# Layer 0 of a four-layer network: VectorE's second operands in PSUM, and the side work of the loop cut into other steps

## The chip, the cores and the metric

The kernel runs on one core of one Trainium2 chip. The metric is the device time of one execution in microseconds (us), lower is better. A core has TensorE (PE, matmuls), VectorE (DVE), ScalarE (ACT), GpSimd (POOL) and queues that start transfers. [...]SBUF is the main on-chip memory[...].

## The reference

The input x has the shape (2, 512, 32, 32). Four layers follow each other. Layer 0 is deformable attention with a position bias, then an MLP; layer 1 is a linear attention, layers 2 and 3 are attention with a group norm. The change touches layer 0 alone. Cut to what matters of it:

```python
xn = bn(x)                                   # (b, 512, 32, 32)
q = gconv1x1(xn, qw)                         # 8 groups of 64 channels
off = depthwise_conv6x6(q, stride 4)         # (b*8, 64, 8, 8): 36 taps
off = tanh(einsum(gelu(off + b), pw)) * 4
vgrid = 2 * (grid + off) / 7 - 1             # 64 sampling points for each group
kv = grid_sample(xn, vgrid)                  # bilinear
k, v = gconv1x1(kv, kw), gconv1x1(kv, vw)
pos = grid_q[:, :, None] - vgrid[:, None]    # 1024 queries x 64 points x 2
bias = sign(pos) * log1p(abs(pos))
bias = relu(bias @ w1 + b1)                  # 2 -> 128
bias = relu(bias @ w2 + b2)                  # 128 -> 128
bias = bias @ w3 + b3                        # 128 -> 1
attn = softmax(q.T @ k * scale + bias)
x = x + out_w @ (attn @ v) + out_b
```

## The kernel before, in words

The heavy part of layer 0 is the bias MLP: 16 heads (2 images x 8) x 1024 queries x 64 points through a 128x128 layer. It runs in a loop over 256 rounds, `quads`: 16 heads `u`, 8 steps `o`, 2 halves `jj`. A round covers four points of a head with all 1024 queries. Below, a round with jj = 0 is called even, one with jj = 1 odd. A pair is two heads that share the 128 partitions; there are eight pairs, so 32 rounds each.

In every round, in this order of the program:

1. `first_hidden` for the *next* round: VectorE writes four tiles' halves `h` of 128 x 1024 (L455, a custom add with saturation, of a row term `x` in SBUF and a column term `y` in PSUM). Every second time, for an even round to come, `table` first writes new `y` (L443). `h` has four buffers of two such halves, so two rounds' worth.
2. `second_hidden` for this round: PE makes four products `hp` (L486), each 128 x 1024 in two PSUM banks of a pool `ps` with three slots. ScalarE takes each out with Relu (L491), ScalarE and GpSimd flip signs (L493, L495, L497, L502), and GpSimd adds them (L504) or starts adding transfers (L478).
3. In even rounds `last_product`: the third layer's product for a pair of rounds that lies back (`sim`, L518).
4. The two queues of side work each take one step, up to the next `yield` of a generator: `after` holds the attention of finished heads (`attend`: ss, then tp with maximum and subtraction, exp, sum with inverse and product, pp/pt, o) and the output projection; `front` holds the preparation of the next pair (`offsets`: xn, q, products with the taps, their reduction `conv`, gelu, tanh, positions, logarithms; `sampled`: transposes, the weights `w` of the sampling, kv, keys and values).

The order on PE, ScalarE, VectorE and GpSimd is that of the program (`manual_schedule`), so a step's instruction stands behind the h of its round, and before the h of the next one.

`bank` is a tile of one PSUM bank, 512 values for each partition. It holds `y` (0 to 256), and for moments the small products: `o` of the offsets (L309, read by tanh, L311), `kv_ps` (L376), `k_ps` and `v_ps` (L389, L391, read at L394 to L397). Lines that the prediction names besides: L263 xn, L281 the copies of q, L288 the products with the taps, L301 their reduction, L352 to L357 the step that makes the distances g, wx and w, L367 to L370 the step that makes the weights of w, L541 ss, L550 and L551 maximum and subtraction, L555 to L557 sum, inverse and product, L565 pt, L617 and L621 the projection.

Of the kernel before, what the change touches and what calls it, by code (L numbers as in the profile page):

```python
# [11 lines left out]
F32 = mybir.dt.float32  # L12
# [40 lines left out]
class Net:  # L53
# [43 lines left out]
    def layer0(self):  # L97
# [3 lines left out]
        with ExitStack() as ctx:  # L101
            keep = self.pool(ctx, "l0")
            self.l0qkv = keep.tile([P, 3, CT, P], F32, tag="qkv", name="qkv")
            nc.scalar.dma_start(self.l0qkv[:, 0], io["l0_qkv"][:, 0])
            nc.scalar.dma_start(self.grid, io["grid"])
            self.l0w2 = keep.tile([P, P], F32, tag="w2", name="w2")
            nc.scalar.dma_start(self.l0w2, io["cpb_w2"])
            self.s1 = self.bn(keep, "bn1")
            self.last_weights(keep)
            nc.scalar.dma_start(self.l0qkv[:, 1:3], io["l0_qkv"][:, 1:3])  # L110
            ow = keep.tile([P, CT, C], F32, tag="ow", name="ow")
            nc.scalar.dma_start(ow, io["out_w"])
# [12 lines left out]
            self.bank = self.pool(ctx, "c_ps_t", 1, psum=True).tile([P, HF], F32, tag="bank", name="bank")  # L125
            ps_s = self.pool(ctx, "c_ps_s", 1, psum=True)

            engines = {getattr(mybir.EngineType, e) for e in ("PE", "Activation", "DVE", "Pool")}
            with self.tc.manual_schedule(engines=engines):
                pairs = [{} for _ in range(BP)]  # L130
                for n, _ in enumerate(self.offsets(pairs[0], 0, ps)):
                    if n == 4:
                        self.fold_weights()
                front = [self.sampled(pairs[0], 0, ps)]
                after, sims, att = [], {}, None
                tables = {}
                quads = [(u, o, jj) for u in range(2 * BP) for o in range(8) for jj in range(2)]
                ready = self.first_hidden(*quads[0], pairs, tables)
                held, self.join = [], None
                for i, (u, o, jj) in enumerate(quads):  # L140
                    if o == 1 and jj == 1 and u % 2 == 0 and u // 2 + 1 < BP:
                        nxt = pairs[u // 2 + 1]
                        front += [self.offsets(nxt, u // 2 + 1, ps), self.sampled(nxt, u // 2 + 1, ps)]
                    h1 = ready
                    if i + 1 < len(quads):
                        if quads[i + 1][1:] == (7, 0) and u + 1 < 2 * BP:
                            self.advance(front, lambda: "logs" in pairs[(u + 1) // 2])
                        ready = self.first_hidden(*quads[i + 1], pairs, tables)
                    z = self.second_hidden(u, o, jj, h1, i + 1 == len(quads))
                    if jj == 1:  # L150
                        held.append((u, o, (first, z)))
                    else:
                        first = z
                        if len(held) == 2:
                            v, last, zs = held.pop(0)
                            self.last_product(v, last, zs, sims, ps_s)
                            if last == 7:
                                if v % 8 == 0:
                                    self.advance(after, lambda: False)
                                    att = [  # L160
                                        apool.tile([P, N], F32, tag=f"att{t}", name=f"att{v}_{t}") for t in range(CT)
                                    ]
                                self.advance(front, lambda: "v" in pairs[v // 2])
                                after.append(self.attend(v, pairs[v // 2], sims.pop(v), att, ps))
                                if v % 8 == 7:
                                    after.append(self.projection(ps, att, ow, v // 8))
                    self.step(after)
                    self.step(front)

                self.join(True)  # L170
                self.advance(after, lambda: False)
                self.last_product(*held[0], sims, ps_s)
                accs = [ps.tile([P, 2, HF], F32, tag="ps", name=f"ob{o}") for o in range(CT - 1)]
                share = self.share(accs, att, ow)
# [59 lines left out]
    def step(behind):  # L234

        while behind:
            for _ in behind[0]:
                return
            behind.pop(0)

    @staticmethod
    def advance(behind, enough):

        while behind and not enough():
            for _ in behind[0]:
                break
# [2 lines left out]

    def projection(self, ps, att, ow, b):  # L250
        for o in range(CT):
            for h in range(2):
                self.project_one(ps, att, ow, "out_b", b, o, h)
                yield

    def offsets(self, m, bt, ps):

# [29 lines left out]
        for ky in range(6):  # L287
# [7 lines left out]
                self.colr("dw_w", len(TAPS))[:, 6 * ky : 6 * ky + 6].unsqueeze(2).unsqueeze(3).to_broadcast([P, 6, 8, 8]),  # L295
                ALU.mult,
            )
            if ky % 3 == 2:
                yield
        conv = self.fpool.tile([P, NJ], F32, tag="conv", name=f"conv{b}{t}")  # L300
        nc.vector.tensor_reduce(conv, prod.rearrange("p a b j -> p j (a b)"), AX.X, ALU.add)  # L301
        yield
        ge = self.fpool.tile([P, NJ], F32, tag="ge", name=f"ge{b}{t}")
        nc.scalar.activation(ge, conv, AF.Gelu, bias=self.col("dw_b"))
        yield
        o = self.bank[:, 256:258]
        for par in range(2):
            rows = slice(par * DH, (par + 1) * DH)
# [27 lines left out]
    def sampled(self, m, bt, ps):  # L336
# [11 lines left out]
        for n in range(NB):  # L348
# [8 lines left out]
        nc.vector.tensor_tensor(  # L357
            w,
            g[:, 1, :].unsqueeze(1).to_broadcast([P, NB, 2 * NJ]),
            self.grid[:, G_Y : G_Y + NB].unsqueeze(2).to_broadcast([P, NB, 2 * NJ]),  # L360
            ALU.subtract,
        )
        yield
        nc.scalar.activation(wx, wx, AF.Abs)
        nc.scalar.activation(w, w, AF.Abs)
        yield
        nc.vector.tensor_scalar(wx, wx, -1.0, 1.0, ALU.mult, ALU.add)  # L367
        nc.vector.tensor_scalar(wx, wx, 0.0, None, ALU.max)
        nc.vector.tensor_scalar(w, w, -1.0, 1.0, ALU.mult, ALU.add)
        nc.vector.scalar_tensor_tensor(w, w, 0.0, wx.unsqueeze(1).to_broadcast([P, NB, 2 * NJ]), ALU.max, ALU.mult)  # L370
        yield
        kv_ps = self.bank[:, 384:448]
        for n in range(NB):
            for par in range(2):
# [13 lines left out]
        k_ps = self.bank[:, 448:512]  # L388
        nc.tensor.matmul(k_ps, lhsT=self.l0qkv[:, 1, t, :], rhs=kv, start=True, stop=True)  # L389
        v_ps = self.bank[0:NJ, 256:384]  # L390
# [135 lines left out]
    def attend(self, u, m, sim, att, ps):  # L526
# [22 lines left out]
        e = self.soft.tile([P, 8, NJ], F32, tag="e", name=f"e{u}")  # L549
        nc.vector.tensor_reduce(st[:, 0, :], tp, AX.X, ALU.max)  # L550
        nc.vector.tensor_tensor(e, tp, st[:, 0, :].unsqueeze(2).to_broadcast([P, 8, NJ]), ALU.subtract)  # L551
        yield
        nc.scalar.activation(e, e, AF.Exp)
        yield
        nc.vector.tensor_reduce(st[:, 1, :], e, AX.X, ALU.add)  # L555
        nc.vector.reciprocal(st[:, 2, :], st[:, 1, :])
        nc.vector.tensor_tensor(e, e, st[:, 2, :].unsqueeze(2).to_broadcast([P, 8, NJ]), ALU.mult)  # L557
        yield
        pp = ps.tile([P, HF], F32, tag="ps", name=f"pp{u}") if ps else self.bank
        for i in range(4):  # L560
            nc.tensor.transpose(
# [987 lines left out]
```

## Time and profile before

| | |
|---|---|
| median of 3 executions | 3453.95 us (3453.79 to 3456.14) |
| profiled execution, span | 3450.1 us |
| TensorE busy | 3394.9 us, 98% |
| VectorE busy | 2313.2 us, 67% |
| ScalarE busy | 2017.4 us, 58% |
| GpSimd busy | 2078.3 us, 60% |
| between 86 and 2066 us (most of layer 0): PE busy | 1975.24 of 1980 us |
| the same stretch: DVE, ACT, POOL busy | 1435.56, 1540.08, 1526.80 us |
| TensorE clock granted | 0.997 |

A line of the groups reads: line of the kernel, engine, operation, output<-input by the program's names, shape, number of records | busy us, mean ns of one | idle time just before them, and what ended most of it. A line of a timeline reads: start us, duration us, engine, line, operation, names, shapes, number of records merged, and in brackets idle time before it with its releaser. A matmul of fp32 leaves two records. The ends of matmuls are modelled: a PE that waits for an operand within a group is drawn as a longer group, which is why the starts are compared.

### The profile page before, as it was taken

What the parts mean: (1) busy time and instruction counts of PE and PEld (TensorE: products, weight loads), DVE (VectorE), ACT (ScalarE), POOL (GpSimd) and SP (SyncE); (2) the same over time, 40 slices, a digit from 0 to 9 for tenths busy, and PEclk for the clock granted to TensorE, in tenths of its full rate; (3) what the DMA queues carried; (4) which work ended last, traced back from release to release, by engine and by line L of the source; (5) the groups of instructions that cost most, each with busy time, mean ns of one, the idle gap of its engine ahead of it and who ended that gap; (6) DMA issues with size and microseconds to landing.
All of it is one profiled execution on the core that took longest, in us unless ns stands there. A gap on an engine that the chain in (4) does not pass through costs nothing.

```text
span 3450.1 us, 60119 instructions
## 1 busy us (share of the span) xinstructions
PE 3394.9 (98%) x25280; PEld 1260.6 (37%) x25280; DVE 2313.2 (67%) x2539; ACT 2017.4 (58%) x2100; POOL 2078.3 (60%) x1584
## 2 busy tenths in 40 slices
PE   7999999999999999999999999999999999999999
PEld 2333333333333333333333334444555433455333
DVE  6877777777767567777776764575556577555774
ACT  5877877887787577877887761111111466113661
POOL 4778777787787577787788874442323444234441
PEclk9999999999999999999999999999989999999999
DMA  6878777877887577887888872111000100000001
GB/s 154 156 144 159 149 155 146 156 158 141 157 161 141 108 156 149 155 157 144 167 168 158 159 152 76 49 37 37 1 1 0 50 1 2 1 0 13 2 1 50
DMA packets 103247, 342.64 MB, mean 99 GB/s; under 512 B 12720, under 2 KB 14384, under 8 KB 100144
## 3 DMA queue, kind: packets, MB, share of 16 engines
q0 software_dynamic: 73296, 266.90, 41.0%
q1 hardware_dynamic: 28656, 69.68, 6.8%
q8 instruction: 202, 3.31, 0.4%
q10 hardware_dynamic: 1008, 2.06, 0.2%
q14 instruction: 85, 0.70, 0.1%
HBM read 67.27 MB, written 4.46 MB: 21 GB/s over the span
## 4 chain that ended last, share of the span: by engine, by line
PE 80%; DVE 15%; ACT 2%; POOL 1%; issue 1%; DMA 0%; DVEq 0%; ACTq 0%; SPq 0%; POOLq 0%
PE hp L486 46%; DVE h L455 3%; PE pb L598 3%; DVE r L1298 3%; PE sim L518 3%; PE o L1275 2%; DVE sum L1262 2%; PE s L1246 2%; PE qk20P L1041 1%; PE qk30P L1041 1%; PE m_0P L649 1%; PE qk21P L1041 1%; PE m_5P L649 1%; PE m_4P L649 1%; PE m_2P L649 1%; PE qk31P L1041 1%
## 5 line engine op out<-in xcount | busy, mean ns | idle before, releaser
L486 PE MATMUL hp<-h,w 128*32 128x512 f32 x16384 | 1831.1, 593 | 5.5 <-DVE h L455 3.6
L455 DVE CUSTOM_DVE_ANT_1 h<-tx,bank 128x1024 f32<-128x1024 f32 x1024 | 1180.4, 1215 | 332.9 <-PE hp L486 310.6
L491 ACT ACTIVATE h<-hp,magb 128x1024 f32<-128x1024 f32 x1024 | 1122.0, 1111 | 416.7 <-PE hp L486 415.6
L486 PEld LDWEIGHTS hp<-h,w 128*32 128x32 f32 x16384 | 543.1, 110 | 1216.1 <-issue 1120.9
L478 POOL DMA_DIRECT2D h<-h x509 | 451.7, 1023 | 392.5 <-ACT h L497 334.0
L504 POOL TENSOR_TENSOR h<-h,h 128x1024 f32<-128x1024 f32 x255 | 613.5, 2406 | 21.3
L502 POOL TENSOR_SCALAR h<-h,flip 128x1024 f32<-128x1024 f32 x256 | 447.7, 1749 | 0.9 <-ACT h L491 0.9
L1250 ACT ACTIVATE e<-s 128x1024 f32<-128x1024 f32 x256 | 258.2, 1024 | 177.6 <-PE s L1246 164.1
L493 ACT ACTIVATE h<-h,flip 128x1024 f32<-128x1024 f32 x256 | 291.3, 1138 | 0.0
L1275 PE MATMUL o<-e,v 64*64 64x512 f32 x2048 | 261.0, 592 | 6.7 <-DVE q L1285 6.7
L1246 PE MATMUL s<-q,k 64*64 64x512 f32 x2048 | 259.8, 589 | 2.6 <-DVE v L1079 1.8
L1257 POOL TENSOR_TENSOR some<-some,e 128x1024 f32<-128x1024 f32 x64 | 151.5, 2367 | 75.7 <-ACT e L1250 73.3
L495 POOL TENSOR_SCALAR h<-h,flip 128x1024 f32<-128x1024 f32 x128 | 144.9, 1132 | 77.4 <-ACT h L491 76.0
L1255 POOL TENSOR_TENSOR some<-e,e 128x1024 f32<-128x1024 f32 x32 | 75.5, 2361 | 190.8 <-DVE sum L1264 155.6
L497 ACT ACTIVATE h<-h,flip 128x1024 f32<-128x1024 f32 x128 | 145.6, 1137 | 0.0
L518 PE MATMUL sim<-h,ends 128*32 128x512 f32 x1024 | 141.0, 592 | 0.0
L1260 DVE TENSOR_TENSOR sum<-e,e 128x1024 f32<-128x1024 f32 x32 | 46.4, 1451 | 136.1 <-ACT e L1250 136.1
L1275 PEld LDWEIGHTS o<-e,v 64*64 64x64 f32 x2048 | 75.8, 133 | 157.3 <-issue 123.7
L1246 PEld LDWEIGHTS s<-q,k 64*64 64x64 f32 x2048 | 78.7, 133 | 143.4 <-issue 117.9
L628 POOL TENSOR_TENSOR mlp_w<-mlp_w 128x512 f32<-128x512 f32 x16 | 22.4, 1401 | 161.0 <-DMA mlp_w<-in_mlp_w 136.7
L708 ACT ACTIVATE mh<-mh,cols 128x512 f32<-128x512 f32 x64 | 46.2, 722 | 124.2 <-DVE mh L726 65.5
L1029 POOL TENSOR_TENSOR sq<-q 128x512 f32<-128x512 f32 x32 | 33.3, 1039 | 139.7 <-DVE q L1048 95.6
(456 smaller groups left out, 3280.2 us busy)
## 6 DMA issues: line engine op xcount, KB each, us to landing
h<-h POOLq DMA_DIRECT2D x509, 512.0 KB, 6.5
lb<-logs SPq DMA_DIRECT2D x63, 512.0 KB, 5.2
mlp_w<-in_mlp_w SPq DMA_DIRECT2D x16, 1024.0 KB, 4.9
x<-in_x SPq DMA_DIRECT2D x8, 512.0 KB, 9.7
qkw<-in_l_qk SPq DMA_DIRECT2D x2, 2048.0 KB, 8.3
out<-x SPq DMA_DIRECT2D x16, 256.0 KB, 2.1
vw<-in_l_v SPq DMA_DIRECT2D x2, 1024.0 KB, 7.4
proj<-in_l_proj SPq DMA_DIRECT2D x8, 256.0 KB, 5.1
```

Source lines behind the costliest of these rows:

```text
L455: self.nc.vector._custom_dve(TENSOR_ADD_SAT, out=h[:, k, :, :], in0=x[:, jj, 2 * r + k, :].unsqueeze(1).to_broadcast([P, H, W]), in1=y[:, ...
L478: nc.gpsimd.dma_start(to, what, accum_op=ALU.add)
L486: nc.tensor.matmul(hp[rows, cut], lhsT=self.l0w2[:, 32 * q : 32 * q + 32], rhs=h1[k][:, cut], start=True, stop=True)
L491: nc.scalar.activation(y, hp, AF.Relu, bias=self.magb[:, q : q + 1])
L493: nc.scalar.activation(ys[0], ys[0], AF.Copy, scale=self.flip[:, 0:1])
L502: nc.gpsimd.tensor_scalar(y, y, self.flip[:, 2:3], 1.0, ALU.mult, ALU.mult)
L504: (nc.vector if final else nc.gpsimd).tensor_tensor(y, y, ys[2], ALU.add)
L518: nc.tensor.matmul(sims[u][at : at + 32, :], lhsT=self.ends[:, 28 - 4 * o : 60 - 4 * o], rhs=z[jj][:, h * HF : (h + 1) * HF], start=(o == ...
L1246: nc.tensor.matmul(s[halves[c], par, :], lhsT=ks[p][rows, at : at + DH], rhs=qs[p][rows, cut], start=True, stop=True)
L1250: nc.scalar.activation(e, s, AF.Exp, scale=DH**-0.5)
L1257: nc.gpsimd.tensor_tensor(state["some"], state["some"], e, ALU.add)
L1275: nc.tensor.matmul(o[halves[par], r, :], lhsT=v[n // 2][rows, n % 2, at : at + DH], rhs=e[rows, par, :], start=(n == 0), stop=(n == NB - 1),)
```

## The change

Five things are edited.

- Operands of VectorE that both lay in SBUF: one of each pair now lies in free columns of `bank`. The taps (36 columns) and the row numbers `ys` (8) are copied there once; `inv`, the inverse of the softmax's sum, and `wp`, the weights along x, are written there by the instruction that makes them. `k_ps` and `v_ps` move to other columns to make room.
- The convolution in parts: the products go two rows of taps to a step instead of three, and their reduction is cut into three instructions with a step each. The last step of the weights `w` is cut in two.
- Two of the attention's steps (those with the maximum and with the sum) give back True, and so does the projection; in such a round the front queue takes no step.
- `odd()`: three steps that use the bank from PE wait, by empty yields, for a round with jj = 1. `advance`, which runs steps in bulk, sets jj to 1 so that it doesn't spin.
- The projection takes both halves of a block in one step with one addition of 1024 columns.

The purpose is that VectorE doesn't wait for GpSimd[...], and that its long steps don't meet in one round. Cut to its core:

```diff
+            self.taps, self.ys = self.bank[:, 320 : 320 + len(TAPS)], self.bank[:, 356 : 356 + NB]
+            self.inv = self.bank[:, 364 : 364 + 8]
+            nc.vector.tensor_copy(self.taps, self.colr("dw_w", len(TAPS)))
+            self.jj = 1
...
-                    if n == 4:
+                    if n == 7:
+                        nc.vector.tensor_copy(self.ys, self.grid[:, G_Y : G_Y + NB])
                         self.fold_weights()
...
+                    self.jj = jj
...
-                    self.step(after)
-                    self.step(front)
+                    if not self.step(after):
+                        self.step(front)
...
-            for _ in behind[0]:
-                return
+            for much in behind[0]:
+                return much
...
+    def odd(self):
+        while self.jj == 0:
+            yield
...
     def projection(self, ps, att, ow, b):
         for o in range(CT):
+            acc = ps.tile([P, 2, HF], F32, tag="ps", name=f"out_b{b}{o}")
             for h in range(2):
-                self.project_one(ps, att, ow, "out_b", b, o, h)
-                yield
+                for t in range(CT):
+                    self.nc.tensor.matmul(acc[:, h, :], ...)
+            self.nc.vector.scalar_tensor_tensor(xt, acc, self.col("out_b", o), xt, ALU.add, ALU.add)
+            yield True
...
-                self.colr("dw_w", len(TAPS))[:, 6 * ky : 6 * ky + 6].unsqueeze(2)...
+                self.taps[:, 6 * ky : 6 * ky + 6].unsqueeze(2)...
-            if ky % 3 == 2:
+            if ky % 2:
                 yield
-        nc.vector.tensor_reduce(conv, prod.rearrange("p a b j -> p j (a b)"), AX.X, ALU.add)
-        yield
+        for third in (slice(0, 24), slice(24, 44), slice(44, NJ)):
+            nc.vector.tensor_reduce(conv[:, third], prod[:, :, :, third].rearrange("p a b j -> p j (a b)"), AX.X, ALU.add)
+            yield
...
+        yield from self.odd()
...
-            self.grid[:, G_Y : G_Y + NB].unsqueeze(2)...
+            self.ys.unsqueeze(2)...
...
+        nc.vector.tensor_scalar(w, w, -1.0, 1.0, ALU.mult, ALU.add)
+        yield
+        wp = self.bank[:, 384:512]
         nc.vector.tensor_scalar(wx, wx, -1.0, 1.0, ALU.mult, ALU.add)
-        nc.vector.tensor_scalar(wx, wx, 0.0, None, ALU.max)
-        nc.vector.tensor_scalar(w, w, -1.0, 1.0, ALU.mult, ALU.add)
-        nc.vector.scalar_tensor_tensor(w, w, 0.0, wx.unsqueeze(1)..., ALU.max, ALU.mult)
+        nc.vector.tensor_scalar(wp, wx, 0.0, None, ALU.max)
+        nc.vector.scalar_tensor_tensor(w, w, 0.0, wp.unsqueeze(1)..., ALU.max, ALU.mult)
...
         nc.vector.tensor_tensor(e, tp, st[:, 0, :]..., ALU.subtract)
-        yield
+        yield True
...
-        nc.vector.reciprocal(st[:, 2, :], st[:, 1, :])
-        nc.vector.tensor_tensor(e, e, st[:, 2, :]..., ALU.mult)
-        yield
+        inv = self.inv if ps else st[:, 2, :]
+        nc.vector.reciprocal(inv, st[:, 1, :])
+        nc.vector.tensor_tensor(e, e, inv..., ALU.mult)
+        yield True
```

More of the change, by code (lines that the diff above doesn't have):

```diff
@@ L236, in step, with advance @@
         while behind:
-            for _ in behind[0]:
-                return
+            for much in behind[0]:
+                return much
             behind.pop(0)
-    @staticmethod
-    def advance(behind, enough):
+    def odd(self):
+        while self.jj == 0:
+            yield
+    def advance(self, behind, enough):
+        self.jj = 1
         while behind and not enough():
@@ L251, in projection @@
         for o in range(CT):
+            acc = ps.tile([P, 2, HF], F32, tag="ps", name=f"out_b{b}{o}")
             for h in range(2):
-                self.project_one(ps, att, ow, "out_b", b, o, h)
-                yield
+                for t in range(CT):
+                    self.nc.tensor.matmul(
+                        acc[:, h, :],
+                        lhsT=ow[:, t, o * P : (o + 1) * P],
+                        rhs=att[t][:, h * HF : (h + 1) * HF],
+                        start=(t == 0),
+                        stop=(t == CT - 1),
+                    )
+            xt = self.xs[b][o].rearrange("p (h x) -> p h x", h=2)
+            self.nc.vector.scalar_tensor_tensor(xt, acc, self.col("out_b", o), xt, ALU.add, ALU.add)
+            yield True
     def offsets(self, m, bt, ps):
@@ L294, in offsets @@
                 ),
-                self.colr("dw_w", len(TAPS))[:, 6 * ky : 6 * ky + 6].unsqueeze(2).unsqueeze(3).to_broadcast([P, 6, 8, 8]),
+                self.taps[:, 6 * ky : 6 * ky + 6].unsqueeze(2).unsqueeze(3).to_broadcast([P, 6, 8, 8]),
                 ALU.mult,
             )
-            if ky % 3 == 2:
+            if ky % 2:
                 yield
         conv = self.fpool.tile([P, NJ], F32, tag="conv", name=f"conv{b}{t}")
-        nc.vector.tensor_reduce(conv, prod.rearrange("p a b j -> p j (a b)"), AX.X, ALU.add)
-        yield
+        for third in (slice(0, 24), slice(24, 44), slice(44, NJ)):
+            nc.vector.tensor_reduce(conv[:, third], prod[:, :, :, third].rearrange("p a b j -> p j (a b)"), AX.X, ALU.add)
+            yield
         ge = self.fpool.tile([P, NJ], F32, tag="ge", name=f"ge{b}{t}")
@@ L359, in sampled @@
             g[:, 1, :].unsqueeze(1).to_broadcast([P, NB, 2 * NJ]),
-            self.grid[:, G_Y : G_Y + NB].unsqueeze(2).to_broadcast([P, NB, 2 * NJ]),
+            self.ys.unsqueeze(2).to_broadcast([P, NB, 2 * NJ]),
             ALU.subtract,
@@ L366, in sampled @@
         yield
+        nc.vector.tensor_scalar(w, w, -1.0, 1.0, ALU.mult, ALU.add)
+        yield
+        wp = self.bank[:, 384:512]
         nc.vector.tensor_scalar(wx, wx, -1.0, 1.0, ALU.mult, ALU.add)
-        nc.vector.tensor_scalar(wx, wx, 0.0, None, ALU.max)
-        nc.vector.tensor_scalar(w, w, -1.0, 1.0, ALU.mult, ALU.add)
-        nc.vector.scalar_tensor_tensor(w, w, 0.0, wx.unsqueeze(1).to_broadcast([P, NB, 2 * NJ]), ALU.max, ALU.mult)
+        nc.vector.tensor_scalar(wp, wx, 0.0, None, ALU.max)
+        nc.vector.scalar_tensor_tensor(w, w, 0.0, wp.unsqueeze(1).to_broadcast([P, NB, 2 * NJ]), ALU.max, ALU.mult)
         yield
+        yield from self.odd()
         kv_ps = self.bank[:, 384:448]
@@ L387, in sampled @@
         yield
-        k_ps = self.bank[:, 448:512]
+        yield from self.odd()
+        k_ps = self.bank[:, 256:320]
         nc.tensor.matmul(k_ps, lhsT=self.l0qkv[:, 1, t, :], rhs=kv, start=True, stop=True)
-        v_ps = self.bank[0:NJ, 256:384]
+        v_ps = self.bank[0:NJ, 384:512]
         nc.tensor.matmul(v_ps, lhsT=kv, rhs=self.l0qkv[:, 2, t, :], start=True, stop=True)
@@ L555, in attend @@
         nc.vector.tensor_reduce(st[:, 1, :], e, AX.X, ALU.add)
-        nc.vector.reciprocal(st[:, 2, :], st[:, 1, :])
-        nc.vector.tensor_tensor(e, e, st[:, 2, :].unsqueeze(2).to_broadcast([P, 8, NJ]), ALU.mult)
-        yield
+        inv = self.inv if ps else st[:, 2, :]
+        nc.vector.reciprocal(inv, st[:, 1, :])
+        nc.vector.tensor_tensor(e, e, inv.unsqueeze(2).to_broadcast([P, 8, NJ]), ALU.mult)
+        yield True
         pp = ps.tile([P, HF], F32, tag="ps", name=f"pp{u}") if ps else self.bank
```

## The prediction

> **What bounds the kernel now.** I read the busy shares, then the chain that ended last, then the costliest groups, and last the timelines of single engines inside layer 0.
>
> ```profile
> PE 3394.9 (98%) x25280; PEld 1260.6 (37%) x25280; DVE 2313.2 (67%) x2539; ACT 2017.4 (58%) x2100; POOL 2078.3 (60%) x1584
> PE 80%; DVE 15%; ACT 2%; POOL 1%; issue 1%; DMA 0%; DVEq 0%; ACTq 0%; SPq 0%; POOLq 0%
> L486 PE MATMUL hp<-h,w 128*32 128x512 f32 x16384 | 1831.1, 593 | 5.5 <-DVE h L455 3.6
> L455 DVE CUSTOM_DVE_ANT_1 h<-tx,bank 128x1024 f32<-128x1024 f32 x1024 | 1180.4, 1215 | 332.9 <-PE hp L486 310.6
> ```
>
> TensorE holds the whole kernel, and layer 0 above all. VectorE's time counts only where TensorE waits for it. The busy share hides that: a matmul that waits for its operand is drawn as a long one. In the chain's own order an undisturbed pair of rounds of the 256-round loop takes 14.59 us (128 hp records 13.73, 8 sim records 0.86), one round's 64 hp records 6.87 to 7.07. The excess over that is the stall. The timelines of PE, then VectorE (DVE), then GpSimd (POOL), at a pair's second collision:
>
> ```profile
> 340.99 0.66 PE L561 MATMUL pp<-ident,e 128*128 128x128 f32 x4
> 341.71 10.36 PE L486 MATMUL hp<-h,w 128*32 128x512 f32 x64
> 351.99 0.66 PE L576 MATMUL o<-pt,v 64*64 64x256 f32 x8
> 360.76 8.24 PE L486 MATMUL hp<-h,w 128*32 128x512 f32 x62
> ```
> ```profile
> 333.96 1.92 DVE L557 TENSOR_TENSOR e<-e,st 128x512 f32<-128x512 f32 x1
> 335.81 4.63 DVE L288 TENSOR_TENSOR prod<-qpad,cols 128x384 f32<-128x384 f32 x3
> 340.35 4.61 DVE L455 CUSTOM_DVE_ANT_1 h<-tx,bank 128x1024 f32<-128x1024 f32 x4
> ...
> 352.97 4.40 DVE L301 TENSOR_REDUCE conv<-prod 128x64 f32<-128x2304 f32 x1
> ```
> ```profile
> 333.57 1.76 POOL L502 TENSOR_SCALAR h<-h,flip 128x1024 f32<-128x1024 f32 x1
> 335.42 2.71 POOL L504 TENSOR_TENSOR h<-h,h 128x1024 f32<-128x1024 f32 x1
> ```
>
> 64 hp records take 10.36 instead of 7.0: 3.4 us lost. VectorE was late with h: e x st (L557, shortest 0.69) took 1.92 beside L502, and three products (L288, shortest 0.82) took 4.63 beside L504. At 360.76 the 4.40 us convolution costs another 1.5, and 0.64 went ahead of the 3.4, where the q copies waited behind ACT's exp. I added such excesses from 90 to 2089 us: 4.8 in pair 0 and 1 (0.94 + 0.84 + 2.98), then 5.6, 5.5, 5.6, 4.6, 5.6, 5.6 for the six later pairs: **37.1 us**. That is all that the change can win inside the loop.
>
> The 2.98 is the case that I use most below. Round 19 has the attention's tp step and the corner weights' step together; hp began at S = 192.0:
>
> ```profile
> 192.84 0.69 DVE L551 TENSOR_TENSOR e<-tp,st 128x512 f32<-128x512 f32 x1
> 193.45 0.39 DVE L367 TENSOR_SCALAR wx<-wx 128x128 f32<-128x128 f32 x1
> 193.88 2.42 DVE L368 TENSOR_SCALAR wx<-wx 128x128 f32<-128x128 f32 x1
> 196.22 0.68 DVE L369 TENSOR_SCALAR w<-w 128x1024 f32<-128x1024 f32 x1
> 196.94 1.23 DVE L370 SCALAR_TENSOR_TENSOR w<-w,wx 128x1024 f32<-128x1024 f32 x1
> 198.08 4.61 DVE L455 CUSTOM_DVE_ANT_1 h<-tx,bank 128x1024 f32<-128x1024 f32 x4
> ```
> ```profile
> 192.00 1.76 POOL L502 TENSOR_SCALAR h<-h,flip 128x1024 f32<-128x1024 f32 x1
> 193.84 2.38 POOL L504 TENSOR_TENSOR h<-h,h 128x1024 f32<-128x1024 f32 x1
> ```
>
> L367 slips in when L502 ends; L368 (0.23 when free) then sits out all of L504. It isn't a pair of tensors: it has one SBUF tensor.
>
> [...]3.02 for a product's longest, 2.42 for L368, while L551, with an operand in PSUM, is 690 to 692 ns in all its 15 runs. [...]So tensor_scalar from SBUF stays exposed, and the change doesn't touch that. [...]L357 shows 1225 to 1226. With PSUM in it L455 takes 1214, so moving an operand has no price of its own.
>
> **The budget of a round.** h for round i+2 can be written only when hp of round i is done, and must be there when hp of i+1 is. Work that waits for PE's last matmul of round i (pt, ss, tp, q) starts at S, the start of the next hp. Until the next hp PE has 7.0 us plus its own step work (0.6 for tp or o) plus 0.86 for sim, if the coming round is even. VectorE needs 4.65 for four h, and 0.45 for L443 if the coming round is odd. That leaves about 2.5 us after an even round and 3.1 or more after an odd one. Work that doesn't wait for S starts some 2.4 earlier.
>
> **The change part by part.** I walked both queues (attention, front) through the 256 rounds by the order of their yields.
> - Operands in PSUM: 48 products, 8 w subtractions, 8 w products, 16 e x inv lose the lock wait. Their floors stay (0.82, 1.23, 1.23, 0.69). The products read every fourth element, which the operand's move leaves as it is. VectorE saves 48 x (1.19 - 0.82) = 18 us, all of it only of use where PE waits.
> - Products two at a time, the convolution in thirds (4.39 becomes 1.6 + 1.4 + 1.4), no front step beside max/subtract and beside sum/inv: no round has over 1.7 of these, under the budget. The 3.4 and 1.5 go.
> - q moves from beside exp to beside pt. Copies end at S + 2.0 (exp's place pushed them to S + 2.4); L443 and h end at S + 7.1 against 7.6. The 0.64 goes, by 0.5 only.
> - wp to PSUM and w in two steps: they fall into rounds of their own. The 2.98 goes.
> - The front's 13 + 8 yields, with the waits for an odd round, still end in time: for pair 2 the table's logs are written in round 50 and needed at 61, v at 61 and needed at 82. No bulk run at a deadline.
> - The odd waits: tanh and v then follow rounds whose next round needs no L443. The waits of L455 for tanh (15.4 us in 5) and of L443 (6.8) are slack already; I give 0.
> - Bank accesses: h (L455) reads the bank ahead of each new reader in the same round, so it has met any wait for ACT or PE before them: 0. PE's writes into the bank queue behind that same h as before.
> - Projection: 4 x 8 matmuls for 8 x 4, PE work the same 3.63 us each half; four changes of tile shape fewer, about 0.1 each: -0.4. One 1.2 us addition (by L455, also 1024 with PSUM) at S is within budget.
> - The start, on the chain: two more reduces, some 0.1 each, +0.2; the taps copy hides behind the qkv load, which the first matmul awaits, the ys copy behind ACT's gelu.
>
> **The new collision.** By the walk, pt (even round) now meets the g step (L352 to L357) in rounds 54, 86, 118, 182 and 214, where before g had rounds of its own (46, 78, ...). Pairs 1 and 5 escape. Before, pt starts at S + 0.1 and the next VectorE work at S + 0.7; L502 runs from S - 0.1 to S + 1.7, L504 from S + 1.75 to S + 4.15 in all such rounds. [...]it waits for L502, ends at S + 2.0, L504 takes the lock to S + 4.3; L354 (0.28) ends at 4.6, L355 at 4.8, w at 5.9; L443 to 6.4, h to 11.0. PE could go on at S + 7.6. **Stall 3.4 us each, 17.0 in all**, the likeness of round 19. Bounds: with no lock wait 0.2 each; with one 1.2 each.
> Likewise round 18, ss beside the at/pos pairs, which stay in SBUF: 0 to 2, I take 1. Round 20 has exp and ln, each with a 1.28 us table load, 3.9 us on ACT: three hp buffers cover about 3, I take 0.9.
>
> **Sum.** Stalls 37.1 become 17.0 + 1 + 0.9 = 18.9: -18.2; projection -0.4, start +0.2: -18.4. 3453.95 - 18.4 = **3435.5**.
>
> **Rivals.**
> - A, the g step is not blocked (POOL's L502 and L504 shift against S): 5 x 0.2 to 1.2 remain: 37.1 - 1 to 6 - 2 gives 29 to 34 saved, 3420 to 3425; take 3422. For it: one g of eight ran in 0.44. Against: the fixed phase above.
> - B, stalls move: q beside pt has 0.5 to spare; if ACT is late by 1.5 in six pairs, 9 return, 3445.
> - C, the bank serialises: L455 shows waits of 3.1 us for a tanh that uses other columns of the bank. If each of 16 inv pairs waited 3.1, +50 against -37 and the 0.2: 3467, slower. Against: h already stands before inv in the same round.
>
> **How the numbers follow.** Main case 0.50, A 0.28, B 0.12, C 0.10. Leaving out C and the far end of B, and widening A for its bounds: 3418 to 3449. Faster by 0.2% means under 3447.0: main, A, and half of B, 0.84; same 0.08; slower 0.08.
>
> **What would show it.** Right: no hp group of over 8 us beside products or convolution; L288 with a mean near 0.82; L557 always 0.69; L354 near 2.5 and hp groups of 10.4 us beside pt at five places, 250 us apart. Wrong: L352 to L355 short there (then A), or VectorE idle before L288 or inv with ACT as releaser (then C).

## The result, and the profile after

The kernel after takes **3430.47 us** (median of 4 executions, 3430.09 to 3431.83) against 3454.11 us (4 executions, 3453.79 to 3456.14): ratio 0.9931, 95% interval 0.9914 to 0.9948. It is faster by 23.6 us; the prediction had 3435.5, within 3418 to 3449.

The busy shares, the shares of the chain that ended last, and the two costliest groups, of the kernel after:

```profile
PE 3376.9 (98%) x25280; PEld 1243.1 (36%) x25280; DVE 2314.8 (68%) x2553; ACT 2020.2 (59%) x2102; POOL 2070.3 (60%) x1584
PE 86%; DVE 11%; ACT 1%; POOL 1%; issue 1%; DMA 0%; DVEq 0%; ACTq 0%
L515 PE MATMUL hp<-h,w 128*32 128x512 f32 x16384 | 1822.1, 593 | 5.3 <-DVE h L484 3.6
L484 DVE CUSTOM_DVE_ANT_1 h<-tx,bank 128x1024 f32<-128x1024 f32 x1024 | 1179.9, 1215 | 276.6 <-PE hp L515 241.1
```

TensorE is busy for 18 us less, and VectorE as long as before: 2314.8 for 2313.2. What moves is who stands on the chain: VectorE holds 11% of it for 15%. VectorE's idle time before h is down from 332.9 to 276.6, but that doesn't measure the gain: it has in the main moved to other steps (the wait of pt for PE alone went from 32.2 to 55.5). In the new numbering hp is L515, h L484, y L472, sim L547, GpSimd's two operations L531 and L533, the products L311, e x inv L587, pt L595, and the g step L377 to L382.

TensorE's timeline in the kernel after, in the rounds where before lost 3.4 us beside three products, and VectorE's next to it:

```profile
339.39 7.07 PE L515 MATMUL hp<-h,w 128*32 128x512 f32 x64
346.39 0.66 PE L606 MATMUL o<-pt,v 64*64 64x256 f32 x8
346.98 7.07 PE L515 MATMUL hp<-h,w 128*32 128x512 f32 x64
```
```profile
346.58 1.65 DVE L311 TENSOR_TENSOR prod<-qpad,bank 128x384 f32<-128x384 f32 x2
```

Two products take 1.65, that is 0.82 each, and each hp group takes the undisturbed 7.07. Over all 48 products, before and after, and 15 of the 16 e x inv after (shortest, median and longest in ns), the median stays and the long cases are gone:

```profile
L288 DVE TENSOR_TENSOR prod<-qpad,cols x48: 823/886/3022, 12.0 to 1625.3; 128x384 f32<-128x384 f32 x48
L311 DVE TENSOR_TENSOR prod<-qpad,bank x48: 814/892/945, 11.9 to 1623.2; 128x384 f32<-128x384 f32 x48
L587 DVE TENSOR_TENSOR e<-e,bank x15: 686/686/691, 203.5 to 1958.0; 128x512 f32<-128x512 f32 x15
```

PSUM is where this kernel's matmuls put their results; GpSimd's two operations of a round read and write h in SBUF. The prediction and the expectations speak of a lock between VectorE and GpSimd; it stands for a wait that the runs show, and what lies behind the wait they don't show. With all tensors in SBUF, beside those two operations, a product took up to 3.02 and e x inv up to 1.93 before; with the taps and the inverse in PSUM no product took over 0.945 and no e x inv over 0.691. For g, a tensor_scalar from SBUF to SBUF, the prediction rests on round 19, where L368, another such instruction, took 2.42 for 0.23 beside L504.

The stall that the prediction expected in their place is there too. TensorE, VectorE and GpSimd in round 54 of the kernel after:

```profile
460.67 7.07 PE L515 MATMUL hp<-h,w 128*32 128x512 f32 x64
467.67 0.66 PE L606 MATMUL o<-pt,v 64*64 64x256 f32 x8
468.30 9.93 PE L515 MATMUL hp<-h,w 128*32 128x512 f32 x63
477.64 0.60 PE L547 MATMUL sim<-h,ends 128*32 128x512 f32 x3
...
493.51 7.45 PE L515 MATMUL hp<-h,w 128*32 128x512 f32 x61
500.90 1.15 PE L404 MATMUL bank<-w,xnT 128*64 128x64 f32 x32
501.98 3.21 PE L515 MATMUL hp<-h,w 128*32 128x512 f32 x28
```
```profile
460.77 0.69 DVE L595 COPY pt<-pp 128x512 f32<-128x512 f32 x1 [3.70 <-PE pp L591]
461.38 1.10 DVE L377 TENSOR_SCALAR g<-at 128x256 f32<-128x256 f32 x1
462.52 2.37 DVE L379 TENSOR_SCALAR wx<-g,grid 128x128 f32<-128x128 f32 x1
464.81 0.21 DVE L380 TENSOR_SCALAR g<-g 128x128 f32<-128x128 f32 x1
465.06 1.22 DVE L382 TENSOR_TENSOR w<-g,bank 128x1024 f32<-128x1024 f32 x1
466.31 0.49 DVE L472 TENSOR_SCALAR bank<-lb,cols 128x256 f32<-128x256 f32 x1
466.93 9.13 DVE L484 CUSTOM_DVE_ANT_1 h<-tx,bank 128x1024 f32<-128x1024 f32 x8
```
```profile
460.58 1.75 POOL L531 TENSOR_SCALAR h<-h,flip 128x1024 f32<-128x1024 f32 x1
462.41 2.39 POOL L533 TENSOR_TENSOR h<-h,h 128x1024 f32<-128x1024 f32 x1
```

g ends at 462.48, just as L533 (462.41) follows on L531 (to 462.33), and wx, 0.29 us of work, sits out all of L533. From the hp start at 468.30 to the sim start at 477.64 are 9.34 us, some 2.5 too many. A second part comes 33 us later: the last hp records of the fourth round and the kv products are late by 0.8. The stretch from 460.67 to 501.98 takes 41.31 against 37.97 for undisturbed work: **3.34 us each**, in rounds 54, 86, 118, 182 and 214 (hp at 468.3, 715.8, 963.2, 1483.7 and 1731.1), 16.7 in all. The sum is the lateness of h: the last of the four that hp at 468.30 needs is written at 471.54 (466.93 and 4.61 for four), 3.24 us after that start.

**The account.** The first product of layer 0's MLP starts at 2089.18 before and at 2069.48 after: 19.7 us of the gain lie in layer 0. The profiled executions differ by 21.2 (spans 3450.1 and 3428.9); the other 1.5 come later, 1.3 of them in layer 1, where a group of ten weight products took 8.29 before and 7.03 after. The change doesn't touch it, and the same group took 4.64, 7.59, 8.41 and 8.81 in four of the runs below. The granted TensorE clock differed there: over the 50 us around the group it was 0.80 before, 0.83 after and 0.93 in the run with 4.64. So it is no part of the effect. The remaining 2.4 of the timed 23.6 come from which executions were profiled: before's, at 3451.91, lay 2.2 under its median, after's, at 3430.73, 0.3 over.

### The profile page after: what moved, and what is told of

Its sections match the earlier page's. It is cut to its first block, busy times and chain, and to the rows that moved or that the text cites. A ratio compares the mean times of both kernels' runs of the same rounds, so it can differ in the third digit from the quotient of the medians.

```text
span 3428.9 us, 60151 instructions
## 1 busy us (share of the span) xinstructions
PE 3376.9 (98%) x25280; PEld 1243.1 (36%) x25280; DVE 2314.8 (68%) x2553; ACT 2020.2 (59%) x2102; POOL 2070.3 (60%) x1584
## 4 chain that ended last, share of the span: by engine, by line
PE 86%; DVE 11%; ACT 1%; POOL 1%; issue 1%; DMA 0%; DVEq 0%; ACTq 0%
PE hp L515 50%; PE pb L628 3%; PE sim L547 3%; DVE r L1328 3%; PE o L1305 2%; DVE sum L1292 2%; PE s L1276 2%; PE qk20P L1071 1%; PE qk30P L1071 1%; PE m_0P L679 1%; PE qk21P L1071 1%; PE m_5P L679 1%; PE m_4P L679 1%; PE m_2P L679 1%; PE qk31P L1071 1%; PE m_6P L679 1%
## 5 line engine op out<-in xcount | busy, mean ns | idle before, releaser
L515 PE MATMUL hp<-h,w 128*32 128x512 f32 x16384 | 1822.1, 593 | 5.3 <-DVE h L484 3.6
L484 DVE CUSTOM_DVE_ANT_1 h<-tx,bank 128x1024 f32<-128x1024 f32 x1024 | 1179.9, 1215 | 276.6 <-PE hp L515 241.1
L515 PEld LDWEIGHTS hp<-h,w 128*32 128x32 f32 x16384 | 530.4, 110 | 1221.4 <-issue 1154.3
L533 POOL TENSOR_TENSOR h<-h,h 128x1024 f32<-128x1024 f32 x255 | 610.2, 2393 | 21.3
L531 POOL TENSOR_SCALAR h<-h,flip 128x1024 f32<-128x1024 f32 x256 | 446.9, 1746 | 0.9 <-ACT h L520 0.9
L1280 ACT ACTIVATE e<-s 128x1024 f32<-128x1024 f32 x256 | 258.4, 1024 | 177.6 <-PE s L1276 167.3
L524 POOL TENSOR_SCALAR h<-h,flip 128x1024 f32<-128x1024 f32 x128 | 144.5, 1129 | 47.9 <-ACT h L520 46.8
L547 PE MATMUL sim<-h,ends 128*32 128x512 f32 x1024 | 142.5, 592 | 0.0
```

The lines of the kernel that those rows point to most:

```text
L484: self.nc.vector._custom_dve(TENSOR_ADD_SAT, out=h[:, k, :, :], in0=x[:, jj, 2 * r + k, :].unsqueeze(1).to_broadcast([P, H, W]), in1=y[:, ...
L515: nc.tensor.matmul(hp[rows, cut], lhsT=self.l0w2[:, 32 * q : 32 * q + 32], rhs=h1[k][:, cut], start=True, stop=True)
L531: nc.gpsimd.tensor_scalar(y, y, self.flip[:, 2:3], 1.0, ALU.mult, ALU.mult)
L533: (nc.vector if final else nc.gpsimd).tensor_tensor(y, y, ys[2], ALU.add)
L547: nc.tensor.matmul(sims[u][at : at + 32, :], lhsT=self.ends[:, 28 - 4 * o : 60 - 4 * o], rhs=z[jj][:, h * HF : (h + 1) * HF], start=(o == ...
L1280: nc.scalar.activation(e, s, AF.Exp, scale=DH**-0.5)
```

## The experiments

Each is timed against the kernel before, in alternation on one chip. Not all ran on the same chip: the medians of the kernel before lay between 3452.84 and 3454.11, so differences between two of the runs below, or from the kernel after, are good to about 1.3 us. "After" as the base of a diff is the kernel after.

### Which half carries the gain

**Operands alone** (before, with the four operands in PSUM and the old steps):

```diff
-  self.colr("dw_w", len(TAPS))[...]   -  self.grid[:, G_Y : G_Y + NB]   -  wx   -  st[:, 2, :]
+  self.taps[...]                      +  self.ys                        +  wp   +  self.inv
```

> The kernel before with the operands in PSUM (taps, ys, wp, inv) and none of the new steps. Theory 'the lock made the long steps long' (both halves of the change cure the same stalls): the products beside the sum step lose their wait for GpSimd, so the 3.4 us stall at six pairs goes nearly or wholly; the 0.64 (q beside exp) stays, the convolution's 1.5 stays within 0.5, and the 2.98 in round 19 stays, since L368 and L369 there have one SBUF tensor. 17 to 21 us less than before, 3433 to 3437. Rival 'only the spreading counts, the sum of VectorE's work in a round is too long with or without lock': 0 to 5 us less, 3449 to 3454.

Measured: 3434.34 us (3432.49 to 3437.57), ratio 0.994 (0.9923 to 0.9957): 19.4 us faster, as expected. VectorE and GpSimd in the same pair as above, of this run:

```profile
335.95 0.69 DVE L563 TENSOR_TENSOR e<-e,bank 128x512 f32<-128x512 f32 x1
336.56 2.48 DVE L292 TENSOR_TENSOR prod<-qpad,bank 128x384 f32<-128x384 f32 x3
338.97 4.58 DVE L460 CUSTOM_DVE_ANT_1 h<-tx,bank 128x1024 f32<-128x1024 f32 x4
```
```profile
335.58 1.76 POOL L507 TENSOR_SCALAR h<-h,flip 128x1024 f32<-128x1024 f32 x1
337.43 2.40 POOL L509 TENSOR_TENSOR h<-h,h 128x1024 f32<-128x1024 f32 x1
```

Inverse product and three products take 0.69 and 2.48 beside the same two GpSimd operations that made them 1.92 and 4.63 before. The 3.4 is gone with no step moved. What stays is 0.64 (q beside exp) and about 1.8 (the whole reduction) in a pair, and 2.86 in round 19. There the expectation had the right loss for a reason that holds only in part. VectorE and GpSimd in that round:

```profile
194.42 0.29 DVE L373 TENSOR_SCALAR bank<-wx 128x128 f32<-128x128 f32 x1
194.63 2.69 DVE L374 TENSOR_SCALAR w<-w 128x1024 f32<-128x1024 f32 x1
```
```profile
194.39 2.38 POOL L509 TENSOR_TENSOR h<-h,h 128x1024 f32<-128x1024 f32 x1
```

L373 is the L368 of before, which took 2.42 at this place; writing to PSUM, it takes 0.29 beside the same GpSimd operation. The wait passes to the next instruction, from SBUF to SBUF, which was 0.68 before.

**Steps alone** (after, with all four operands back in SBUF):

```diff
-  self.taps[...]   -  self.ys                    -  wp = self.bank[:, 384:512]   -  inv = self.inv if ps else st[:, 2, :]
+  self.colr(...)   +  self.grid[:, G_Y : ...]    +  wp = wx                      +  inv = st[:, 2, :]
```

> The changed kernel with its operands back in SBUF (taps, ys, wp, inv), all steps and odd waits as changed. Theory 'both halves cure the same stalls': a pair of products in a round of its own can wait once for GpSimd (up to 2.4 us) and still be in time; 3430 to 3434, within 3 us of the changed kernel. Rival 'the PSUM operands carry the gain': 15 us or more above the changed kernel, 3445 or more.

Measured: 3455.91 us (12 executions, 3454.26 to 3456.76), ratio 1.0005 (0.9996 to 1.0014): nothing won. **The theory fell, the rival held.** VectorE and GpSimd of this run:

```profile
346.83 5.72 DVE L309 TENSOR_TENSOR prod<-qpad,cols 128x384 f32<-128x384 f32 x2
...
356.99 3.85 DVE L309 TENSOR_TENSOR prod<-qpad,cols 128x384 f32<-128x384 f32 x2
...
366.25 3.69 DVE L309 TENSOR_TENSOR prod<-qpad,cols 128x384 f32<-128x384 f32 x2
```
```profile
347.29 1.75 POOL L529 TENSOR_SCALAR h<-h,flip 128x1024 f32<-128x1024 f32 x1
349.13 2.75 POOL L531 TENSOR_TENSOR h<-h,h 128x1024 f32<-128x1024 f32 x1
```

Cutting three products to two doesn't shorten the wait. The first goes ahead when L529 ends (349.04), the second sits out L531 (to 351.88): two waits in a chain of two, as in before's chain of four (e x inv and three products, 1.92 and 4.63). Three rounds in a row now lose waits: 22 of the 48 products take about 2.9 us, where before six took 3.0. PE's hp pair at 354.98 is 3.7 us longer than 13.7. On top come the five collisions of g, so this run shows that the steps win nothing as they stand, and not what they would win without those.

**The taps alone back in SBUF** (after, one line of the edit above):

> The changed kernel with the taps alone back in SBUF; inv, ys and wp stay in PSUM. The kernel with all four back in SBUF took 3455.9. Theory 'of the four operands the taps carry the gain, as the products of two rows, each with an operand pair, meet L531 and then L533 in one round': 3448 to 3455. Rival 'inv carries it' (its product waited 1.2 us in each of seven heads before): within 6 us of the changed kernel, 3436 or less.

Measured: 3457.15 us (12 executions, 3452.33 to 3458.17), ratio 1.001 (1.0001 to 1.0019), 2 us above the expected range and, within the spread, the same as with all four in SBUF. The source line of the products in this run:

```profile
L310 DVE TENSOR_TENSOR prod<-qpad,cols x48: 825/1175/2945, 12.2 to 1650.0; 128x384 f32<-128x384 f32 x48
```

The longest is 2945 ns for 945. So of the four operands the 36 taps carry what the operands bring beside the new steps; the counterpart, with the taps alone in PSUM, stands below. With the old steps, where e x inv waited in the same round as the products, no run moves the taps alone.

### The new collision

**pt with no front step beside it** (after, in `attend`):

```diff
   nc.vector.tensor_copy(pt, pp)
-  yield
+  yield True
```

> The changed kernel, with the pt step giving back True too, so that no front step runs beside it; g then runs beside o. Theory 'pt beside g costs 3.3 us at five places, because g and L379 wait for GpSimd after pt had waited for PE': the five hp groups of 9.3 us go, 15 to 17 us less than the changed kernel, 3413 to 3416; q now stands beside o, up to 0.4 us at six places. Rival 'the stalls follow the work wherever it stands': less than 5 us less, 3426 or more.

Measured: 3415.77 us (3415.72 to 3416.26), ratio 0.9888 (0.9872 to 0.9905): 14.7 us under the kernel after. Two lines of this run's VectorE timeline, and two of TensorE's, at the place of the collision:

```profile
466.42 0.34 DVE L377 TENSOR_SCALAR g<-at 128x256 f32<-128x256 f32 x1
466.80 0.29 DVE L379 TENSOR_SCALAR wx<-g,grid 128x128 f32<-128x128 f32 x1
```
```profile
467.57 0.66 PE L606 MATMUL o<-pt,v 64*64 64x256 f32 x8
468.16 7.07 PE L515 MATMUL hp<-h,w 128*32 128x512 f32 x64
```

g and wx now run as a GpSimd operation ends (at 466.61) and in the gap behind it, at 0.34 and 0.29 instead of 1.10 and 2.37, and hp takes 7.07. All five stalls are gone; those of rounds 18 and 20 are left (0.95 and 1.56).

**The same five meetings, but the waiting instructions changed**: g stays beside pt, while wx and w become scalar_tensor_tensor with an operand in PSUM, and L380 is folded into w:

```diff
-  nc.vector.tensor_scalar(wx, g[:, 0, :], -0.5, self.grid[:, G_X : G_X + 1], ALU.add, ALU.subtract)
-  nc.vector.tensor_scalar(g[:, 1, :], g[:, 1, :], -0.5, None, ALU.add)
+  nc.vector.scalar_tensor_tensor(wx, g[:, 0, :], -0.5, self.gx.to_broadcast([P, 2 * NJ]), ALU.add, ALU.subtract)
-  nc.vector.tensor_tensor(...)
+  nc.vector.scalar_tensor_tensor(..., -0.5, ..., ALU.add, ...)
```

> The changed kernel with the g step left beside pt, [...]L379 and w become operations with an operand in PSUM (a column with the x of the rows joins the bank), the subtraction L380 falls into w. Only g (L377) can still wait. Theory 'the five stalls are [...]g for L531 and L379 for L533': g ends at S + 2.0, w at S + 3.5, h at S + 8.7 against 7.6; the stall goes from 3.3 to about 1 us, and the follower of 0.85 goes: 10 to 13 us less than the changed kernel, 3417 to 3421. Rival 'the stall comes from the work beside pt': one short instruction of 0.2 us fewer, so 1 us less, 3429 or more.

Measured: 3419.66 us (3416.31 to 3420.84), ratio 0.9905 (0.9888 to 0.9921): 10.8 under the kernel after, or 9.5 when each is set against the kernel before on its own chip. In the profiled executions, of which this one was the fastest of its four, layer 0's MLP starts 11.3 us earlier than in the kernel after (2058.21 for 2069.48). VectorE and TensorE in round 54 of this run:

```profile
461.38 1.10 DVE L379 TENSOR_SCALAR g<-at 128x256 f32<-128x256 f32 x1
462.51 0.29 DVE L381 SCALAR_TENSOR_TENSOR wx<-g,bank 128x128 f32<-128x128 f32 x1
462.72 1.21 DVE L385 SCALAR_TENSOR_TENSOR w<-g,bank 128x1024 f32<-128x1024 f32 x1
...
464.58 9.13 DVE L489 CUSTOM_DVE_ANT_1 h<-tx,bank 128x1024 f32<-128x1024 f32 x8
```
```profile
468.26 7.61 PE L520 MATMUL hp<-h,w 128*32 128x512 f32 x63
498.55 1.15 PE L409 MATMUL bank<-w,xnT 128*64 128x64 f32 x32
```

g waits for its one GpSimd operation as before (1.10); wx runs in 0.29 beside the next (462.41 to 464.80). So most of the stall is the wait of wx for GpSimd's second operation (2.37 for 0.29), and not the length of the step. One part of the expectation missed: the lateness of about 0.8 at the kv products, which was to go with the stall, stayed. It is no cost of its own. The last h is 0.93 late here (464.58 and 4.61, against 468.26), and the stretch up to the hp after kv, 460.67 to 499.63, is 38.96 for 37.97, 0.99 too long; in the kernel after these were 3.24 and 3.34. What is paid beside hp and what at kv adds up to the lateness of h in both.

**ss, exp and pt with no front step**, and **ss and pt alone**:

> The changed kernel, with ss, exp and pt giving back True as well, so that only o (copies on ScalarE) has a front step beside it. Theory: the five places and rounds 18 and 20 (2.5 us together) are free, 17 to 20 us less than the changed kernel, 3410 to 3414. Rival 'the front queue comes too late for its deadlines': a bulk run of steps ahead of a head, with one stall of 10 us or more for each pair, 3440 or more.

> The changed kernel with ss and pt alone in their rounds, exp with a front step beside it. Theory: the 3.3 us at five places go, and the 1.4 us of round 18 (positions beside ss); exp and ln no longer meet in round 20, which frees 1.1: 3412 to 3415, about as the kernel in which exp stands alone too (3413.8). Rival: q beside exp brings back its 0.64 at six pairs: 3417 or more.

Measured: 3413.76 us (3412.48 to 3414.87), ratio 0.9882 (0.9866 to 0.9899), and 3411.96 us (3408.73 to 3412.78), ratio 0.988 (0.9863 to 0.9896). The first came out as expected, the second a hair below its range. The second beats both kernels: 18.5 us under after, some 41 under before. From its second round on, no stall of over 0.3 us is left in the loop. The line of busy times and the hp group on its page:

```profile
PE 3358.6 (99%) x25280; PEld 1247.1 (37%) x25280; DVE 2294.3 (67%) x2553; ACT 2019.6 (59%) x2102; POOL 2072.2 (61%) x1584
L515 PE MATMUL hp<-h,w 128*32 128x512 f32 x16384 | 1798.3, 593 | 4.0 <-DVE h L484 3.6
```

hp is down from 1822.1 to 1798.3 with the mean still 593: the union of its records is shorter, since none waits within a group.

**No waits for odd rounds** (the run with pt alone, and `odd` empty):

```diff
   def odd(self):
-      while self.jj == 0:
-          yield
+      yield from ()
```

> The kernel with pt alone in its round (3415.8), without the waits for an odd round: tanh, kv and keys may now stand in even rounds, whose next round has to write y first. Theory 'the waits of h and y for tanh and v were slack': tanh ends about S + 1, y and h at S + 6.1 against 7.0 or more, so within 1.5 us of 3415.8. Rival 'the odd waits take away stalls': 1.5 to 3 us for each of seven pairs, 3426 or more.

Measured: 3415.13 us (3413.55 to 3415.49), ratio 0.9889 (0.9873 to 0.9906), against 3415.77 with them. The odd waits are worth nothing here.

### What is left of the parts, on the best version

**Only the taps in PSUM** (ss and pt alone; the inverse, ys and wp back in SBUF):

> The kernel with ss and pt alone in their rounds (3412.0), with only the taps in PSUM; inv, ys and wp are back in SBUF. Theory 'the taps alone carry the gain of the operands': w subtractions and products [...]were never kept waiting before; e x inv can wait up to 2 us, but its round has no front step beside it: 3410 to 3416. Rival 'the other three count once the taps are free': 3419 or more.

Measured: 3413.03 us (3412.65 to 3413.67), ratio 0.9882 (0.9865 to 0.9898), 1.1 above 3411.96, with overlapping spreads; against the kernel before on its own chip each wins 41 us. The other three operands bring at most about 1 us together. The trace of before agrees: in its loop only six products and six e x inv were kept waiting, while the w subtractions (L357) and w products (L370) took 1.22 to 1.23 in all cases.

**The convolution** in three forms on the same version:

```diff
-  if ky % 2:                          (first and third form: products by three)
+  if ky % 3 == 2:
-  for third in (slice(0, 24), slice(24, 44), slice(44, NJ)):      (first and second form: reduction whole)
-      nc.vector.tensor_reduce(conv[:, third], ...)
-      yield
+  nc.vector.tensor_reduce(conv, ...)
+  yield
```

> The kernel with ss and pt alone in their rounds (3412.0), with the products three rows of taps to a step and the reduction whole, as before the change. Theory 'the convolution cost 1.5 us only as VectorE came to it late from the products[...]': its 4.4 us start 2.4 ahead of S and end at S + 2.0, within the budget of 2.5: 3410 to 3416. Rival 'an instruction of 4.4 us is too long for any round': 1.5 us for seven pairs, 3421 or more.

> The kernel with ss and pt alone (3412.0), products two rows to a step as there, the reduction whole in one step. With three rows to a step and the reduction whole it took 3425.6. Theory 'lateness adds up over neighbouring rounds': products of 1.65 us stay under the 2.2 us that a round leaves on average, so the 4.4 us find VectorE in time and end at S + 2.0: 3410 to 3416. Rival 'the whole reduction is too long in itself': 3421 or more.

> The kernel with ss and pt alone (3412.0), products three rows to a step (2.5 us, 0.3 over what a round leaves), the reduction in thirds. Theory 'lateness adds up': 0.3 twice, made good in the thirds: 3410 to 3416. Rival 'the products by three are what stalls': 3421 or more.

| products | reduction | us | ratio (95%) |
|---|---|---|---|
| by two | thirds | 3411.96 (3408.73 to 3412.78) | 0.988 (0.9863 to 0.9896) |
| by three | whole | 3425.62 (3424.45 to 3426.64) | 0.9918 (0.9901 to 0.9934) |
| by two | whole | 3411.82 (3409.33 to 3413.99) | 0.988 (0.9864 to 0.9897) |
| by three | thirds | 3413.5 (3412.32 to 3414.01) | 0.9884 (0.9868 to 0.9901) |

With both uncut, **the theory fell** (3410 to 3416 expected): 13.6 us are lost, 12.5 with each set against the kernel before on its own chip. VectorE, then TensorE, in one pair of that run:

```profile
121.91 2.49 DVE L311 TENSOR_TENSOR prod<-qpad,bank 128x384 f32<-128x384 f32 x3
129.62 2.47 DVE L311 TENSOR_TENSOR prod<-qpad,bank 128x384 f32<-128x384 f32 x3
136.53 4.43 DVE L324 TENSOR_REDUCE conv<-prod 128x64 f32<-128x2304 f32 x1
```
```profile
137.55 15.22 PE L514 MATMUL hp<-h,w 128*32 128x512 f32 x127
```

No product waits for GpSimd (three take 2.47 to 2.49), yet hp's two rounds take 15.22 for 13.9. Either cut alone is enough, so it isn't the length of the reduction by itself: steps of 2.5, 2.5 and 4.4 us in three neighbouring rounds add up, as the expectations of the second and third form had said.

## Why the prediction was right

**Direction, size and mechanism held.** It put the stalls left at 18.9 us: 17.0 beside g, 1 in round 18, 0.9 in round 20. The trace has 16.7 and, over rounds 18 to 21, 2.5 (182.35 to 214.90: 32.55 us against 30.02, which the run with ss and pt alone takes there), together 19.2. The gain within layer 0 is 19.7 for 18.4. The 1 and 0.9 were picked within wide bounds, so that they come so near is in part luck.

- **The old stalls go.** L311 has a median of 892 ns (814 to 945), a little over the 0.82 given; L587 is at its floor in every case with PSUM; no hp group is long beside the products, the reduction or q. The operands-alone run shows that the operand does this (no product over 925 ns), and the steps-alone run that the steps without it win nothing (products up to 2937), their g collisions included.
- **The new collision.** Places, rounds and price were as worked out by the walk of the two queues; the run with pt alone takes out 14.7 us, and changing the waiting instructions alone 10.8. Its shape was different: hp beside it takes 9.3, not 10.4, and the rest is paid at the next kv step. The reckoning holds all the same: h was to end at S + 11.0 and PE to be ready at S + 7.6, and with S = 460.67 they did so at S + 10.9 and S + 7.6. L377's three values (327/1104/1201) show that g was the one that met GpSimd's first operation; pairs 1 and 5 escaped as predicted.
- **Round 18** (1 given): pos took 2.29 behind GpSimd's addition, about 1.4 of stall. **Round 20** (0.9 given): about 1.1, from the two table loads of 1.28 us on ACT, the second of them in the front's step, as its timeline in the kernel after shows:

```profile
200.48 1.28 ACT L582 ACT_TABLE_LOAD   x1
202.57 1.28 ACT L350 ACT_TABLE_LOAD   x1
```

With pt alone the two show as 0.95 and 1.56 by the starts of hp, so only their sum of 2.5 is firm.

- **q beside pt** (the 0.64 goes, by 0.5 only) held: no stall there. **Odd waits** 0: held. **Bank accesses** 0, rival C: no inverse product waited, 686 to 691 ns.
- **Mis-sized terms.** The projection gave about 1.3 instead of 0.4: eight steps of 3.63 became four of 7.07, and four changes of tile shape fell away, at 0.13 each (hp takes 7.00 ahead of another product and 6.87 ahead of hp). The start cost some 0.7 instead of 0.2, all of it in the first hp group, which begins at 35.24 for 35.28; but that group differs by 1.1 between runs of kernels that share this part, so no cause is shown. The addends of the 37.1 give 37.3 as they are printed, which rounding can explain. The stalls' fall of 17.9 (37.1 to 19.2), 1.3 from the projection and -0.7 from the start leave 1.2 of the 19.7: small losses spread over the loop, for which the prediction had no term and which I didn't trace one by one.
- **Readings that were wrong without harm to the sum.** VectorE was to save 18 us by 48 products that lose a wait. Their mean before was 1.145 and not 1.19, only six of them waited, and after it is 0.888: 12 us, which longer waits elsewhere (of wx above all) and the reduction in thirds use up again. And the change does touch one tensor_scalar from SBUF, the one that writes wp to PSUM; it isn't exposed any more (0.29 for 2.42, above).
- **Outside it**: the 1.5 after layer 0 and the 2.4 from the choice of executions, above. Within layer 0 the forecast was 1.3 us off; with these two it is 5.2 off the gain of 23.6.

Rival A (g not blocked, 3422) needs wx short in round 54; it took 2.37. Rival B (stalls beside q, 3445) needs a late q; there is none.

**What stays open.** Why the second part of a g stall is paid at kv is not shown. The kernel writes the products of each of the four h to 32 partitions of their own (form 128*32 in the trace). After the stall hp and sim records come interleaved (x3, x1, x4, x3, x1), and the kv products, of the form 128*64, start 0.8 late. My reading is that the products of the four h run out of step and kv waits for the last of them; the two sums above fit it. The 32 matmuls of a round's hp leave 64 records; taken two by two, these are in the order of the program, hp's last product beside sim's first three, then sim's fourth beside the next hp's first three. That is an order of starts; the ends are modelled. No run tests the reading alone. Nor was "steps without the operands and without the g collision" tried.

## What to carry to other kernels

Where instructions of one engine wait for those of another, look at the chain of instructions that wait, not at their time: here one of them slipped in when a GpSimd operation ended (1.10 for g), and the next sat out the whole of the following one (2.37 for wx, 0.29 of work), so cutting three products into two saved nothing (3455.91 us, ratio 1.0005). Free every instruction of the chain: with the taps in PSUM no product took over 0.945, but with only the first of two tensor_scalars freed the wait passed to the second (2.69 for 0.68). When side work is spread over more rounds, walk every queue anew: the shift made a short step (g) meet the one round where GpSimd's two operations held it up, and gave back 17 of 37 us. Judge slack over neighbouring rounds: steps that each fit lost time in a row of three (15.22 for 13.9).

## What the runs showed of the hardware

- **A waiting VectorE instruction went ahead between two GpSimd operations.** g ended at 462.48, 0.15 after L531 (to 462.33) and as L533 began (462.41), on which wx then waited to 464.8. GpSimd's operation was longer too where a product had gone ahead: L531 of the steps-alone run took 2.75 for 2.39.
- **With its destination in PSUM, a tensor_scalar from SBUF didn't wait.** L396 after, from SBUF to PSUM, took 294 to 296 ns in all its 8 cases, and six of them ran beside a GpSimd operation that had begun before: four beside L440 (as at 484.27), one each beside L524 (251.41) and L533 (1746.58). L395, from SBUF to SBUF just ahead of it, took 582/1640/1846. The operands-alone run has the same instruction at the same place with only its destination changed: 0.29 for 2.42.
- **A stall on PE was partly paid later**, some 33 us on in round 54, at the kv products (128*64 beside hp's 128*32): 0.8 of 3.34 in the kernel after, and 0.8 of 0.99 where h was only 0.93 late.
